# Graph attention layer on sorted edges: four weight and sum buffers, small PSUM operands in one bank, batches of 24 groups

## The chip, the cores and the metric

The kernel runs on one core of one Trainium2 chip. The metric is the device time of one execution in microseconds (us). The kernel before takes 4106.01 us, the median of three runs (4105.14 to 4106.99). A separate execution was taken with the hardware profiler; its times are its own and are given below.

## The reference: what is computed

There are 12,500 nodes with 64 features, and 400,000 edges with 64 features each. The edges are sorted by destination. For every edge an attention score is taken from source, destination and edge features; the scores are normalized by a softmax over all edges that arrive at the same node; the messages are summed with these weights; and each node is updated:

```python
z_att = concat([x[src], x[dst], efeats])
e     = leaky_relu(z_att @ W_attn + b_attn, 0.01)
m     = concat([x[src], efeats]) @ W_ne
alpha = softmax of e over the edges of each dst      # segment max, exp, segment sum
z     = segment_sum(alpha * m, dst)
out   = layernorm(x + relu(concat([x, z]) @ W_out))
```

Because the message is linear, the kernel sums the weighted raw features per node and multiplies by W_ne only at the end.

## The kernel before, in words

**Tiling.** 512 edges are a *group* (128 partitions times T = 4 edges); there are 782 groups. SG = 4 groups are a *chunk*, the unit of loads, scores and sums. BG = 32 groups are a *batch*, the unit of the softmax: its rows are laid out as 128 rows of 128 edges, so at most 32 groups fit. The sizes of the batches are a list: 30, then 23 times 32, then 12 and 4. There are 196 chunks.

**A chunk's load** (`gather`, L134). The edge features `ze` come by one DMA on SP's queue (L140). The source rows `zx` come by one indirect DMA for each 128 edges, 16 for a chunk, all issued by GpSimd, which the profile calls POOL (L149). In the first batch they come from x itself, in all later ones from `table`, a copy of x with the source's share of the score as 65th column. A chunk's `ze` and `zx` live in one of ZB = 11 buffers until the chunk is summed.

**A chunk's score** (`scores`, L155). Sorted destinations fall into a window of S = 48 slots. A matmul (L161) spreads the window's destination scores over 128 partitions into the PSUM tile `win`. VectorE multiplies the edge features by `w_edge`, which lies in the PSUM tile `fixed`, and reduces (L165, L167); adds the source's share (L172, the first to need the gathers); builds the one-hot `hot` of the slots (L174), which also lie in `fixed`; picks the destination's share by product and reduction (L179, L182); and writes the scores `y` (L183, L184). In the first batch the source's share is computed on the way (L169, L171). `hot` has HB = 9 buffers.

**A batch's softmax** (`softmax`, L224). The scores are transposed (L252), and a segmented maximum and sum run as scans along rows. Between rows they pass through the tensor engine: a column becomes one row (`to_row`, L190), is scanned, and goes back (`to_col`, L195 to L200). The result is transposed (L307), and ScalarE writes it to the PSUM tile `alpha` (L309), 128 x 4 x 32.

**A chunk's sums** (`aggregate`, L321). VectorE multiplies `hot` by `alpha` into the edge weights `w` (L324, two buffers); the tensor engine multiplies features by weights, 64 matmuls of 128x64 by 128x48 a chunk, into `pg` (L332, two PSUM banks); VectorE adds each group's 48 columns into the accumulator `acc` at the group's first destination (L342). From the third batch on, `own_part` runs after a chunk until 25 pieces are done: it computes x times W_out for four blocks of 128 nodes, through `pg` as well.

**Start and end.** Before the loop VectorE and ScalarE prepare `table`; the windows' scores are written to `wins` by seven indirect DMAs on POOL (`wk`, L422), which stand among the gathers of the first chunks in POOL's queue. The score of the first chunk waits for the last of them, since its buffers take over their memory. After the last batch, `finish_sorted` (L491) applies the weights, relu and layernorm.

**Order.** The program is written batch by batch: score all chunks, softmax, sum all chunks. A scheduler then orders the instructions on each engine by its own estimates and inserts the semaphores; each engine runs its list strictly in order. Two accesses of different engines to one PSUM tile that lies in one bank are ordered against each other, except where both only read, whatever their columns. [...]before, `fixed`, `pp` (index transposes), `win` and `alpha` hold one each, `sm` (softmax rows) two and `pg` two.

Of the kernel before, what the change touches and what calls it, by code (L numbers as in the profile page):

```python
# [9 lines left out]
F32 = mybir.dt.float32  # L10
# [5 lines left out]
P = 128  # L16
T = 4
# [8 lines left out]
S = 48  # L26
BG = 32
SG = 4
HQ = 4
EW = 65  # L30
ZB = 11
HB = 9
NBC = 4

BF16 = mybir.dt.bfloat16
# [3 lines left out]
def sorted_path(ctx, tc, x, dst, idx, edge, w_ne, w_attn, b_attn, w_out, out, flag):  # L39
# [7 lines left out]
    N, D = x.shape  # L47
# [43 lines left out]
    feats = loop.enter_context(tc.tile_pool(name="feats", bufs=ZB))  # L91
    psum = loop.enter_context(tc.tile_pool(name="psum", bufs=2, space=bass.MemoryType.PSUM))

    fixed = psum.tile([P, S + 2 * D], F32, name="fixed", bufs=1)
    slots = fixed[:, 0:S]
    w_edge = fixed[:, S:S + D].unsqueeze(1)
    w_src = fixed[:, S + D:S + 2 * D].unsqueeze(1)

    def indices(g0, G):

# [33 lines left out]
    def gather(g0, n, srcs, b0, plain):  # L134

        ze = feats.tile([P, SG, T, D], F32, name="ze")
        zx = feats.tile([P, SG, T, EW], F32, name="zx")
        whole = min(n, NG - 1 - g0)
# [16 lines left out]
    def scores(g0, n, ze, zx, drel, b0, y, plain):  # L155

        b = g0 - b0
        wrow = tiny.tile([1, SG, S], F32, name="wrow")
        nc.sync.dma_start(out=wrow[:, 0:n, :], in_=wins[g0:g0 + n, :].unsqueeze(0))
        win = psum.tile([P, SG, S], F32, name="win", bufs=1)  # L160
        nc.tensor.matmul(win[:, 0:n, :], ones_row, wrow[:, 0:n, :], start=True, stop=True)  # L161

        yb = y[:, :, b:b + n].rearrange("p t g -> p g t")
        prod = work.tile([P, SG, T, D], F32, name="prod", bufs=1)
        nc.vector.tensor_tensor(prod[:, 0:n], ze[:, 0:n],  # L165
                                w_edge.unsqueeze(1).to_broadcast([P, n, T, D]), op=OP.mult)
        nc.vector.tensor_reduce(yb, prod[:, 0:n], axis=AX.X, op=OP.add)  # L167
        if plain:
            nc.vector.tensor_tensor(prod[:, 0:n], zx[:, 0:n, :, 0:D],  # L169
                                    w_src.unsqueeze(1).to_broadcast([P, n, T, D]), op=OP.mult)  # L170
            nc.vector.tensor_reduce(zx[:, 0:n, :, D], prod[:, 0:n], axis=AX.X, op=OP.add)  # L171
        nc.vector.tensor_tensor(yb, yb, zx[:, 0:n, :, D], op=OP.add)  # L172
        hot = work.tile([P, SG, T, S], BF16, name="hot", bufs=HB)
        nc.vector.tensor_tensor(  # L174
            hot[:, 0:n], slots.unsqueeze(1).unsqueeze(1).to_broadcast([P, n, T, S]),
            drel[:, :, b:b + n].rearrange("p t g -> p g t").unsqueeze(3).to_broadcast([P, n, T, S]),
            op=OP.is_equal)
        at = work.tile([P, SG, T, D], F32, name="prod", bufs=1)[:, :, :, 0:S]
        nc.vector.tensor_tensor(at[:, 0:n], hot[:, 0:n],  # L179
                                win[:, 0:n].unsqueeze(2).to_broadcast([P, n, T, S]), op=OP.mult)  # L180
        sdst = tiny.tile([P, SG, T], F32, name="sdst")
        nc.vector.tensor_reduce(sdst[:, 0:n], at[:, 0:n], axis=AX.X, op=OP.add)  # L182
        nc.vector.tensor_tensor(sdst[:, 0:n], sdst[:, 0:n], yb, op=OP.add)  # L183
        nc.vector.scalar_tensor_tensor(yb, sdst[:, 0:n], SLOPE, sdst[:, 0:n], op0=OP.mult, op1=OP.max)  # L184
        return hot
# [17 lines left out]
    def neighbours(g0, G):  # L203
# [5 lines left out]
        n = G - 1 if last else G  # L209
        for h in range(HQ):  # L210
            r0 = 0
# [12 lines left out]
    def softmax(G, y, d3, carry, first):  # L224


        R = HQ * G
        far = rows.tile([P, P + 2], F32, name="far3")
# [29 lines left out]
        top = tiny.tile([1, P + 1], F32, name="top")  # L258
# [30 lines left out]
        den = tiny.tile([1, P + 1], F32, name="den")  # L289
# [15 lines left out]
                                sm.rearrange("r (q t) -> r q t", t=T), op=OP.mult)  # L305
        alpha0 = rows.tile([P, T, BG], F32, name="alpha0")
        nc.vector.transpose(alpha0.rearrange("p t g -> p (t g)"), al.rearrange("r t q -> r (t q)"))  # L307
        alpha = psum.tile([P, T, BG], F32, name="alpha", bufs=1)
        nc.scalar.activation(alpha, alpha0, AF.Copy)  # L309
        fac = None  # L310
        if not first:
# [4 lines left out]
            nc.tensor.matmul(pfac[:, 0:1], ones_row, fac1, start=True, stop=True)  # L316
            fac = tiny.tile([P, 1], F32, name="fac")
            nc.vector.tensor_copy(fac, pfac[:, 0:1])
        return alpha, fac, (top[:, R:R + 1], den[:, R:R + 1])

    def aggregate(g0, n, ze, zx, hot, alpha, b0, fac):  # L321
        b = g0 - b0
        w = work.tile([P, SG, T, S], F32, name="w")
        nc.vector.tensor_tensor(  # L324
            w[:, 0:n], hot[:, 0:n],
            alpha[:, :, b:b + n].rearrange("p t g -> p g t").unsqueeze(3).to_broadcast([P, n, T, S]),
            op=OP.mult)
        pg = psum.tile([P, SG, P], F32, name="pg")[:, :, 0:S]
        for g in range(n):
            for t in range(T):  # L330
                for at, z in ((0, ze), (D, zx)):
                    nc.tensor.matmul(pg[at:at + D, g, :], z[:, g, t, 0:D], w[:, g, t, :],  # L332
                                     start=(t == 0), stop=(t == T - 1))
        _, vs = nc.values_load_multi_w_load_instructions(
            d0i[0:1, g0:g0 + n], engines=(EngineType.DVE,), min_val=0, max_val=N - 1,
            skip_runtime_bounds_check_because=within)
        for g in range(n):
            if g == 0 and fac is not None:
                a1 = acc[:, ds(vs[0], 1)]
                nc.vector.tensor_scalar(a1, a1, fac, None, op0=OP.mult)  # L340
            ag = acc[:, ds(vs[g], S)]
            nc.vector.tensor_tensor(ag, ag, pg[:, g, :], op=OP.add)  # L342


    sizes = []
    left = NG
    for short in (SG, 3 * SG):
        sizes.insert(0, short)
        left -= short
    while left > 0:  # L350
        sizes.insert(0, min(left, BG))
        left -= sizes[0]
    starts = [sum(sizes[:k]) for k in range(len(sizes))]

# [22 lines left out]
    with tc.tile_pool(name="pre", bufs=2) as pre:  # L377
        d0f = pre.tile([1, NG], F32, name="d0f", bufs=1)
        nc.vector.tensor_copy(d0f, d0i)
        for g0 in range(0, NG, 3 * P):  # L380
            n = min(3 * P, NG - g0)
# [3 lines left out]
        for c0 in range(0, NB, CB):  # L385
            c1 = min(c0 + CB, NB)
            f1 = min(c1, NFULL)
            n = c1 - c0
# [37 lines left out]
    work = loop.enter_context(tc.tile_pool(name="work", bufs=2))  # L426
# [5 lines left out]
    def own_part(c0):  # L432

        n = min(NBC, NB - c0)
        xb = work.tile([P, NBC, D], F32, name="xb", bufs=1)
        if c0 + n > NFULL:
            nc.vector.memset(xb[:, n - 1, :], 0.0)
            nc.scalar.dma_start(out=xb[0:TAIL, n - 1, :], in_=x[NFULL * P:N, :])
        nf = min(n, NFULL - c0)
        if nf:  # L440
            nc.scalar.dma_start(out=xb[:, 0:nf, :],
                                in_=x[c0 * P:(c0 + nf) * P, :].rearrange("(b p) f -> p b f", p=P))
        xtt = work.tile([D, NBC, P], F32, name="xtt", bufs=1)
        pxt = psum.tile([P, NBC, P], F32, name="pg")
        for j in range(n):
            nc.tensor.transpose(pxt[0:D, j, :], xb[:, j, :], ident)
        nc.scalar.activation(xtt[:, 0:n, :], pxt[0:D, 0:n, :], AF.Copy)  # L447
        po = psum.tile([P, NBC, P], F32, name="pg")[:, :, 0:D]
        for j in range(n):
            nc.tensor.matmul(po[:, j, :], xtt[:, j, :], wout[:, 0, :], start=True, stop=True)  # L450
        xo = work.tile([P, NBC, D], F32, name="xo", bufs=1)
        nc.scalar.activation(xo[:, 0:n, :], po[:, 0:n, :], AF.Copy)
        nc.scalar.dma_start(out=early[c0 * P:(c0 + n) * P, :].rearrange("(b p) f -> p b f", p=P),
                            in_=xo[:, 0:n, :])
# [5 lines left out]
    with loop:  # L460
        carry = None
        own = 0
        ready = {k: prepare(k) for k in range(2)}
        for k, G in enumerate(sizes):
            b0 = starts[k]
            srcs, drel = ready.pop(k)
            d3 = neighbours(b0, G)
            y = rows.tile([P, T, BG], F32, name="y", bufs=2)
            if G < BG:
                nc.vector.memset(y[:, :, G:BG], 0.0)  # L470
            parts = []
            for g0 in range(b0, b0 + G, SG):
                n = min(SG, b0 + G - g0)
                ze, zx = ahead.pop(0) if ahead else gather(g0, n, srcs, b0, k == 0)
                hot = scores(g0, n, ze, zx, drel, b0, y, k == 0)
                parts.append((g0, n, ze, zx, hot))
            if k + 2 < len(sizes):
                ready[k + 2] = prepare(k + 2)
            alpha, fac, carry = softmax(G, y, d3, carry, k == 0)
            for g0, n, ze, zx, hot in parts:  # L480
                aggregate(g0, n, ze, zx, hot, alpha, b0, fac if g0 == b0 else None)
                if own < NB and k > 1:
                    own_part(own)
                    own += NBC
        while own < NB:
            own_part(own)
            own += NBC
# [518 lines left out]
```

## Time and profile before

| | |
|---|---|
| median of three runs | 4106.01 us |
| the profiled execution's own time | 5109.14 us |
| its span, first to last instruction | 5107.4 us |
| tensor engine (PE), matmuls | 1410.6 us busy, 28% |
| VectorE (DVE) | 1708.1 us busy, 33% |
| ScalarE (ACT) | 109.6 us busy, 2% |
| GpSimd (POOL) | 2964.9 us busy, 58% |
| mean granted TensorE clock | 0.547 |
| chain that ended last, by engine | issue 28%, POOL 26%, unknown 19%, DVE 14%, PE 10% |

A line of the timeline gives start, duration, engine, line, operation, output and inputs, and in brackets the idle time of the engine before it with what ended that. A line of the waits gives who waited for whom: total, times and longest, in us. "issue" means that the engine waited for nothing that the profile shows; "remote" means that the releaser is not known. The profiled execution is 1003 us longer than the plain runs.

### The profile page before, as it was taken

What the parts mean: (1) busy time and instruction counts of PE and PEld (TensorE: products, weight loads), DVE (VectorE), ACT (ScalarE), POOL (GpSimd) and SP (SyncE); (2) the same over time, 40 slices, a digit from 0 to 9 for tenths busy, and PEclk for the clock granted to TensorE, in tenths of its full rate; (3) what the DMA queues carried; (4) which work ended last, traced back from release to release, by engine and by line L of the source; (5) the groups of instructions that cost most, each with busy time, mean ns of one, the idle gap of its engine ahead of it and who ended that gap; (6) DMA issues with size and microseconds to landing.
All of it is one profiled execution on the core that took longest, in us unless ns stands there. A gap on an engine that the chain in (4) does not pass through costs nothing.

```text
span 5107.4 us, 39846 instructions
## 1 busy us (share of the span) xinstructions
PE 1410.6 (28%) x14238; PEld 1105.0 (22%) x14238; DVE 1708.1 (33%) x4006; ACT 109.6 (2%) x239; POOL 2964.9 (58%) x3142
## 2 busy tenths in 40 slices
PE   0022233443222222222222222222222222222226
PEld 0012122332222122212121212122222211221225
DVE  3333233232342332332323323323233233233346
ACT  0000000000000000000000000000000000000001
POOL 6645656556556556565565565655655655656550
PEclk9975555555555555555555555555555555555555
DMA  6111122222111112111111111111111211212113
GB/s 145 25 34 42 44 48 54 53 53 60 41 45 44 43 38 48 42 46 41 43 44 43 42 44 43 43 42 44 47 41 40 47 42 38 47 37 48 41 36 77
DMA packets 315273, 239.73 MB, mean 47 GB/s; under 512 B 160576, under 2 KB 264235, under 8 KB 315064
## 3 DMA queue, kind: packets, MB, share of 16 engines
q0 software_dynamic: 100320, 104.41, 10.6%
q1 hardware_dynamic: 147464, 116.22, 8.0%
q10 hardware_dynamic: 67280, 16.45, 1.6%
q8 instruction: 115, 1.88, 0.2%
q14 instruction: 94, 0.77, 0.1%
HBM read 226.98 MB, written 12.28 MB: 47 GB/s over the span
## 4 chain that ended last, share of the span: by engine, by line
issue 28%; POOL 26%; another core or an unknown queue 19%; DVE 14%; PE 10%; DMA 3%; DVEq 1%; ACT 0%; POOLq 0%; ACTq 0%
POOL zx L149 26%; PE pg L332 7%; DMA zx<-table,srcs 2%; DVE y L167 2%; DVE prod L165 2%; DVE sdst L182 1%; DVE prod L179 1%; PE sm L198 1%; PE sm L190 1%; DVE hot L174 1%; DVE w L324 1%; DVE by_row L195 0%; DVE b L271 0%; DVE acc L342 0%
## 5 line engine op out<-in xcount | busy, mean ns | idle before, releaser
L149 POOL DMA_INDIRECT zx<-table,srcs x3008 | 2840.6, 944 | 1951.4 <-issue 841.3
L332 PE MATMUL pg<-w,ze 128*64 128x48 f32 x6256 | 792.3, 297 | 1640.2 <-issue 985.1
L332 PEld LDWEIGHTS pg<-w,ze 128*64 128x64 f32 x6256 | 703.6, 213 | 1729.3 <-issue 1581.7
L332 PE MATMUL pg<-w,zx 128*64 128x48 f32 x6256 | 803.4, 297 | 613.2 <-issue 582.1
L324 DVE TENSOR_TENSOR w<-hot,alpha 128x768 f32<-128x768 bf16 x196 | 184.0, 949 | 2208.2 <-remote 1135.9
L332 PEld LDWEIGHTS pg<-w,zx 128*64 128x64 f32 x6256 | 706.7, 213 | 656.3 <-issue 621.7
L342 DVE TENSOR_TENSOR acc<-acc,pg 128x48 f32 x782 | 153.9, 197 | 812.7 <-remote 742.1
L161 PE MATMUL win<-wrow,ones_row 1*128 1x192 f32 (+1 forms) x392 | 182.0, 552 | 746.8 <-DVE prod L179 433.1
L161 PEld LDWEIGHTS win<-wrow,ones_row 1*128 1x128 f32 x392 | 92.9, 284 | 810.4 <-DVE prod L179 448.3
L165 DVE TENSOR_TENSOR prod<-ze,fixed 128x1024 f32<-128x1024 f32 x196 | 236.9, 1209 | 19.9 <-issue 19.9
L167 DVE TENSOR_REDUCE y<-prod 128x16 f32<-128x1024 f32 x196 | 236.1, 1205 | 2.4 <-DVE y L184 2.3
L182 DVE TENSOR_REDUCE sdst<-prod 128x16 f32<-128x768 f32 x196 | 185.1, 944 | 4.3 <-DVE prod L179 2.4
L179 DVE TENSOR_TENSOR prod<-hot,win 128x768 f32<-128x768 bf16 x196 | 185.4, 946 | 0.9 <-issue 0.2
L174 DVE TENSOR_TENSOR hot<-fixed,drel 128x768 bf16<-128x768 f32 x196 | 185.6, 947 | 0.0
L149 POOL DMA_INDIRECT zx<-in_x_dram,srcs x120 | 116.9, 974 | 51.5 <-issue 36.3
L112 ACT ACTIVATE nat<-raw 32x1024 f32<-32x1024 int32 (+3 forms) x26 | 27.5, 1056 | 3242.2 <-PE pp L115 1762.9
L450 PE MATMUL pg<-wout,xtt 64*128 64x64 f32 x196 | 47.4, 418 | 132.0 <-ACT xtt L447 132.0
L198 PE MATMUL sm<-ones_row,by_row 1*128 1x1 f32 x208 | 59.2, 351 | 81.2 <-DVE by_row L195 66.2
L198 PEld LDWEIGHTS sm<-ones_row,by_row 1*128 1x128 f32 x208 | 50.9, 302 | 131.5 <-DVE by_row L195 104.2
L190 PE MATMUL sm<-order,b 128*1 128x128 f32 x104 | 30.1, 391 | 163.8 <-DVE b L271 158.4
L450 PEld LDWEIGHTS pg<-wout,xtt 64*128 64x128 f32 x196 | 42.8, 319 | 148.3 <-ACT xtt L447 148.3
L190 PE MATMUL sm<-order,s 128*1 128x128 f32 x104 | 30.3, 393 | 147.7 <-issue 57.1
(133 smaller groups left out, 949.1 us busy)
## 6 DMA issues: line engine op xcount, KB each, us to landing
ze<-in_edge_dram SPq DMA_DIRECT2D x194, 512.0 KB
zx<-table,srcs POOLq DMA_INDIRECT x3008
table<-xt ACTq DMA_DIRECT2D x14, 227.5 KB
wrow<-wins SPq DMA_DIRECT2D x195, 0.8 KB
xb<-in_x_dram ACTq DMA_DIRECT2D x24, 128.0 KB
early<-xo ACTq DMA_DIRECT2D x24, 128.0 KB
xb<-in_x_dram ACTq DMA_DIRECT2D x12, 256.0 KB
xo<-early SPq DMA_DIRECT2D x12, 256.0 KB
```

The lines of the kernel that those rows point to most:

```text
L149: nc.gpsimd.indirect_dma_start(out=zx[:, g, t, 0:D] if plain else zx[:, g, t, :], out_offset=None, in_=x[:, :] if plain else table[:, :], ...
L161: nc.tensor.matmul(win[:, 0:n, :], ones_row, wrow[:, 0:n, :], start=True, stop=True)
L165: nc.vector.tensor_tensor(prod[:, 0:n], ze[:, 0:n], w_edge.unsqueeze(1).to_broadcast([P, n, T, D]), op=OP.mult)
L167: nc.vector.tensor_reduce(yb, prod[:, 0:n], axis=AX.X, op=OP.add)
L174: nc.vector.tensor_tensor(hot[:, 0:n], slots.unsqueeze(1).unsqueeze(1).to_broadcast([P, n, T, S]), drel[:, :, b:b + n].rearrange("p t g -> ...
L179: nc.vector.tensor_tensor(at[:, 0:n], hot[:, 0:n], win[:, 0:n].unsqueeze(2).to_broadcast([P, n, T, S]), op=OP.mult)
L182: nc.vector.tensor_reduce(sdst[:, 0:n], at[:, 0:n], axis=AX.X, op=OP.add)
L190: nc.tensor.matmul(p[0:1, :], col, order, start=True, stop=True)
L198: nc.tensor.matmul(p[:, 0:1], by_row, ones_row[:, 0:1], start=True, stop=True)
L324: nc.vector.tensor_tensor(w[:, 0:n], hot[:, 0:n], alpha[:, :, b:b + n].rearrange("p t g -> p g t").unsqueeze(3).to_broadcast([P, n, T, S]) ...
L332: nc.tensor.matmul(pg[at:at + D, g, :], z[:, g, t, 0:D], w[:, g, t, :], start=(t == 0), stop=(t == T - 1))
L342: nc.vector.tensor_tensor(ag, ag, pg[:, g, :], op=OP.add)
```

## The change

- The tiles `win` and `alpha` are no longer PSUM tiles of their own. `fixed` is widened to a whole bank (512 columns) and holds slots, `w_edge`, `w_src`, `alpha` and `win` side by side.
- The two banks that this frees go to `pg`, which has four buffers; `w` has four as well.
- A batch has BS = 24 groups (six chunks). The layout of the softmax keeps its 32 places; the last 8 hold zeros. The sizes are 32 times 24, then 10 and 4. There are still 196 chunks, and 34 batches instead of 26.
- ZB goes from 11 to 10 and HB from 9 to 8.

```diff
+BS = 24
-ZB = 11
-HB = 9
+ZB = 10
+HB = 8
...
-    fixed = psum.tile([P, S + 2 * D], F32, name="fixed", bufs=1)
+    fixed = psum.tile([P, 512], F32, name="fixed", bufs=1)
...
+    alpha = fixed[:, S + 2 * D:S + 2 * D + T * BG].rearrange("p (t g) -> p t g", t=T)
+    win = fixed[:, S + 2 * D + T * BG:S + 2 * D + T * BG + SG * S].rearrange("p (g s) -> p g s", g=SG)
...
-        win = psum.tile([P, SG, S], F32, name="win", bufs=1)
...
-        alpha = psum.tile([P, T, BG], F32, name="alpha", bufs=1)
         nc.scalar.activation(alpha, alpha0, AF.Copy)
...
-        w = work.tile([P, SG, T, S], F32, name="w")
+        w = work.tile([P, SG, T, S], F32, name="w", bufs=4)
...
-        pg = psum.tile([P, SG, P], F32, name="pg")[:, :, 0:S]
+        pg = psum.tile([P, SG, P], F32, name="pg", bufs=4)[:, :, 0:S]
...
-    for short in (SG, 3 * SG):
+    for short in (SG, 10):
         sizes.insert(0, short)
         left -= short
     while left > 0:
-        sizes.insert(0, min(left, BG))
+        sizes.insert(0, min(left, BS))
         left -= sizes[0]
```

The two tiles of `own_part` that share the name `pg` get the same `bufs=4`, and `alpha` is no longer passed from `softmax` to `aggregate`.

More of the change, by code (lines that the diff above doesn't have):

```diff
@@ L318, in softmax, with aggregate @@
             nc.vector.tensor_copy(fac, pfac[:, 0:1])
-        return alpha, fac, (top[:, R:R + 1], den[:, R:R + 1])
-    def aggregate(g0, n, ze, zx, hot, alpha, b0, fac):
+        return fac, (top[:, R:R + 1], den[:, R:R + 1])
+    def aggregate(g0, n, ze, zx, hot, b0, fac):
         b = g0 - b0
-        w = work.tile([P, SG, T, S], F32, name="w")
+        w = work.tile([P, SG, T, S], F32, name="w", bufs=4)
         nc.vector.tensor_tensor(
@@ L443, in own_part @@
         xtt = work.tile([D, NBC, P], F32, name="xtt", bufs=1)
-        pxt = psum.tile([P, NBC, P], F32, name="pg")
+        pxt = psum.tile([P, NBC, P], F32, name="pg", bufs=4)
         for j in range(n):
@@ L447, in own_part @@
         nc.scalar.activation(xtt[:, 0:n, :], pxt[0:D, 0:n, :], AF.Copy)
-        po = psum.tile([P, NBC, P], F32, name="pg")[:, :, 0:D]
+        po = psum.tile([P, NBC, P], F32, name="pg", bufs=4)[:, :, 0:D]
         for j in range(n):
@@ L478, in sorted_path @@
                 ready[k + 2] = prepare(k + 2)
-            alpha, fac, carry = softmax(G, y, d3, carry, k == 0)
+            fac, carry = softmax(G, y, d3, carry, k == 0)
             for g0, n, ze, zx, hot in parts:
-                aggregate(g0, n, ze, zx, hot, alpha, b0, fac if g0 == b0 else None)
+                aggregate(g0, n, ze, zx, hot, b0, fac if g0 == b0 else None)
                 if own < NB and k > 1:
```

## The prediction

> **What bounds the kernel now.** I read the page's busy shares first, then the waits of POOL, then the timeline at the start, in a middle batch and at the end. The profiled execution took 5109.1 us (span 5107.4), the plain runs 4106.0, so the first question is what the profile adds.
>
> ```profile
> PE 1410.6 (28%) x14238; PEld 1105.0 (22%) x14238; DVE 1708.1 (33%) x4006; ACT 109.6 (2%) x239; POOL 2964.9 (58%) x3142
> ...
> L149 POOL DMA_INDIRECT zx<-table,srcs x3008 | 2840.6, 944 | 1951.4 <-issue 841.3
> ```
>
> No engine is near full; POOL, which issues one indirect gather for each 128 edges, comes closest. Its waits:
>
> ```profile
> POOL zx L149 <- issue: 877.5, 2825, 8.4
> POOL zx L149 <- PE pg L332: 786.6, 62, 61.1
> POOL zx L149 <- remote: 252.8, 80, 3.8
> ```
>
> The 877.5 us over 2825 gathers is 0.3 us each: the fixed gap between two gathers. The other two, 1039 us, wait for a buffer that the tensor engine (L332) has to free. They resemble the 1003 us by which the profiled run is too long. Why is PE late? The timeline:
>
> ```profile
> 2410.62 0.24 PE L332 MATMUL pg<-w,ze 128*64 128x48 f32 x1 [1.16 <-issue]
> 2411.32 0.24 PE L332 MATMUL pg<-w,zx 128*64 128x48 f32 x1 [0.46 <-issue]
> 2412.02 0.24 PE L332 MATMUL pg<-w,zx 128*64 128x48 f32 x1 [0.46 <-issue]
> ...
> 2412.17 0.31 PE L332 MATMUL pg<-w,ze 128*64 128x48 f32 x1
> 2412.18 0.31 PE L332 MATMUL pg<-w,zx 128*64 128x48 f32 x1
> 2412.27 0.31 PE L332 MATMUL pg<-w,ze 128*64 128x48 f32 x1
> ```
>
> Sometimes the matmuls come 0.70 us apart and wait for nothing, then a pair takes 0.11 us; a chunk of 64 lasts 3.7 us in one place and 17 in another. VectorE shows the same 0.7 us grid at 223 to 262 us. I take this for the cost of being recorded. Without it a chunk (4 groups, 16 gathers) costs POOL 16 x 1.2485 = 20.0 us (31 gathers from 2522.80 to 2561.51), PE 3.7 and VectorE about 7: **POOL's gathers set the time**, if nothing stops them.
>
> The sum for the plain run. Start:
>
> ```profile
> 196.79 1.22 DVE L165 TENSOR_TENSOR prod<-ze,fixed 128x1024 f32<-128x1024 f32 x1 [19.88 <-issue]
> ...
> 204.73 1.21 DVE L165 TENSOR_TENSOR prod<-ze,fixed 128x1024 f32<-128x1024 f32 x1
> ```
>
> ```profile
> 237.59 0.95 POOL L149 DMA_INDIRECT zx<-table,srcs  x1 [0.30 <-issue]
> 299.67 0.94 POOL L149 DMA_INDIRECT zx<-table,srcs  x1 [61.13 <-PE pg L332]
> ```
>
> POOL fills all 11 buffers (168 gathers) by 238.5 and stands until the first softmax has let PE free one. Scoring advances 7.93 us a chunk, but the starts from 220.59 to 268.40 are 16.1 us later than that pace: recording. So the true restart is 299.7 - 16.1 = 283.6. The other 2960 gathers: 2960 x 1.2485 = 3695.6, to 3979.2. Tail: 2.3 us for the last rows to land, then from L172 at 4993.11 to the last addition at 5036.5, 43.4, then 70.9 to 5107.4: 116.6. Total 4095.8, and 1.7 outside the span: 4097.5 against 4106.0. The sum misses 8.5 us, which I carry along.
>
> **The change, part by part.**
>
> *Number of gathers:* 3128 before and after (96 rather than 120 from x): zero.
>
> *Batches of 24: steady state.* Before, the built order puts the score of the next batch's second chunk (L172) inside the softmax, ahead of the first weights:
>
> ```profile
> 2510.93 0.19 DVE L172 TENSOR_TENSOR y<-y,zx 128x16 f32<-128x16 f32 x1
> ```
>
> Counting from T, the end of a batch's last gather, that instruction can run at T + 40 + 2.3; 11.7 us later (2510.93 to 2522.6) PE frees the first buffer, at T + 54, and POOL needs it at T + 60 (3 buffers ahead): 6 us to spare, no stall. Afterwards nothing of the next batch stands in the softmax; the row at T + 4.5 is transposed, softmax takes 16.7 (from the timeline: transpose to the first column copy 3.7; from the scan at 2504.43 to the weights at 2517.83 13.4, of which 0.4 is that L172), weights and matmuls 4.7, so a buffer is free at T + 26, and with 10 buffers and 6 chunks POOL needs it at T + 80. No stall either. Worth 0; if the 8.5 us are small stalls of the old order in its 24 batches, they go: 0 to -8.5. I take 0, since the rows show slack.
>
> *Eight more softmaxes (34 for 26):* 8 x 16.7 = 134 us of VectorE, also 8 x 8 transposes at L115 (0.29), and on SP's queue 8 more index loads and 32 more of dst; hidden under 119.9 us of gathers a batch. Uncovered, they would add the whole 134.
>
> The Trainium skill (SBUF — State Buffer, "Who interferes with whom") speaks against them: copies and tensor_scalar in VectorE's two-port modes take the port on which GpSimd builds descriptors, and block it. By the rule, 0.20 (L236) and four 0.26 copies (L195) a softmax, 8 x 1.24 = 10 us. The row: 3008 gathers total 2840.6 at a median of 0.944, thus 1 us above the median in all; 8/26 of it is 0.3. I take 0.3, keeping 10 as the end.
>
> *One bank for the small operands.* In the new order each L165 waits for PE's window product, and that product waits for VectorE's last read of the bank, the previous batch's weights among them. So scoring of a batch now begins only after the batch before is weighted, and on PE after its matmuls (outside the batches that also carry x times W_out, where it slips in after the third chunk). The Trainium skill (PSUM — Partial Sum Buffer, "PSUM bank collisions raise a hardware error") demands just this: two engines on one bank and quadrant are to be kept apart by semaphores whatever their addresses. Within a batch it costs nothing visible:
>
> ```profile
> 203.66 1.00 PE L161 MATMUL win<-wrow,ones_row 1*128 1x192 f32 x2 [43.60 <-issue]
> ```
>
> It ends at 204.66, and L165 follows at 204.73 anyhow. By address alone scoring could overlap the matmuls as before; by the rule a batch becomes a serial chain: softmax 16.7, first weights 0.95, six chunks of matmuls 22.1, window 1.0, six scores at 5.3 = 31.8 (L165 and L167 at 1.13, L174, L179 and L182 at 0.87 from start to start, small ones 0.4), end 2.1: 74.7 us against 119.9 of gathers. Both give the same time; the cover is 45 us a batch.
>
> *Four buffers of w and pg:* VectorE's 1136 + 1033 us of waiting at L324 shrink; it was not on POOL's path in the plain run: 0. The 25 x W_out pieces between chunks (four transposes, 0.59 on ScalarE, four matmuls: about 3.1 us) make such a batch's matmuls 41 us, still inside.
>
> *Start.* The last window gather, whose landing starts scoring, is POOL's 134th instead of 138th: 5.0 earlier, 191.8. Six chunks to the transpose: 6 x 7.93 + 1.3 = 48.9, to 240.7; softmax 16.7 + 0.3 = 17.0, to 257.7; weights and matmuls 5.0 (294.7 to 299.67): restart at 262.7, 20.9 earlier. But 160, not 168, gathers are done: + 8 x 1.2485 = 10.0. Net **-10.9**. Were the stretch real, it would be 16.1 before and some 8.5 after: -18.5. So -11 to -18; I take -10.9.
>
> *Tail.* Batches 24, 10, 4; the 10 and the 4 take 69.9 us of gathers after T. Serial: transpose T + 4.5, weights T + 21.5, matmuls to T + 44.5, window T + 45.6, scores 5.3 + 5.3 + 3.1 to T + 59.4, softmax 17 to T + 76.4, 2.5 chunks 10.2 to T + 86.6, window and score 6.3 to T + 92.9, softmax 17, last sums 5.4, to T + 115.3, finish 70.9: T + 186.2, so 116.3 after the last gather. Against 116.6: -0.3. With 2 us of error a batch: -3 to +6.
>
> Sum: 262.7 + 2968 x 1.2485 = 3968.2; + 116.3 + 1.7 = 4086.2; + the unexplained 8.5 + 0.3 = **4095.0**, -0.27%.
>
> **The rivals.**
> *A, more is gained:* the 8.5 us are stalls of the old order with only 6 us of slack, and the stretch is real. For it: the thin slack. Against: every row says slack. 4095 - 8.5 - 7.5 = 4079.
> *B, no change:* the start gain is lost in a tail that is serial now (+6) and in the port (+5 to +10). For it: three softmaxes follow each other there. 4095 + 11 = 4106.
> *C, slower:* the serial chain overtakes the gathers. Place: the six chunks of L332 between softmax and window. It decides at 3.7 + 45 / 6 = 11.2 us a chunk. For it: the profile itself has chunks of 14 to 18 us, and before, eight such chunks (20 us each) stayed hidden, so the old plain time can't exclude 12. Against: 0.11 us a pair wherever the stream is not on the 0.7 us grid. At 12.5 us: 6 x 1.3 = 7.8 a batch, 32 batches: +250, 4345.
>
> **How the numbers follow.** Main case 0.46 (4087 to 4104, of which 0.41 under the bound), A 0.15, B 0.22, C and smaller slowdowns (a stall of a few us a batch somewhere) 0.17. This kernel's runs lie within 0.05%; 0.2% (8.2 us) is about what can be told from no change. Faster (below 4097.8): 0.41 + 0.15 = 0.56. Slower: 0.17 + 0.02 of B's upper end = 0.19. Same: 0.25. Predicted 4095; range 4077 to 4118, which takes in A and B and leaves most of C out.
>
> **What would show it.** Right: POOL's pace again 0.94 + 0.30; its first long wait 10 to 25 us shorter than 61; 34 softmaxes; the first product of a score (L165 here, L167 in the new file) late by under 0.2 us within a batch; the last gather to the end near 137 in the profile. The profiled run should stay near 5100 to 5300, since PE's records (now 1% more) fill it; that says nothing of the time. Wrong: a POOL gap at each batch in a part where matmuls run at 0.11 a pair, or a pace other than 1.2485.

## The result, and the profile after

The changed kernel takes **4081.11 us** (median of four runs, 4080.19 to 4082.37), the kernel before beside it 4106.20 (4105.14 to 4106.99). The ratio is 0.9939, with a 95% interval of 0.9922 to 0.9957: 25.1 us, or 0.61%, are gained. The profiled execution took 4080.57 us, its span is 4078.8. So the 1003 us of the first profile of before are no toll that every recorded execution pays.

The page of the changed kernel, the busy times and the gathers:

```profile
PE 985.2 (24%) x14494; PEld 766.8 (19%) x14494; DVE 1875.2 (46%) x4448; ACT 131.6 (3%) x287; POOL 2967.8 (73%) x3142
...
L152 POOL DMA_INDIRECT zx<-table,srcs x3032 | 2866.8, 946 | 956.7 <-issue 869.6
```

POOL is busy 73% of the span, and the fixed gap between two gathers fills most of the rest. The waits of the changed kernel (who waited for whom: total, times, longest) say the same:

```profile
POOL zx L152 <- issue: 898.3, 2947, 0.3
POOL zx L152 <- DMA zx<-table,srcs: 33.2, 109, 0.3
POOL zx L152 <- PE pg L333: 33.2, 2, 32.9
POOL zx L152 <- DVE srcs L121: 15.2, 1, 15.2
```

Only two waits of a gather are longer than 0.3 us. The one of 15.2 stands before the very first gather, in every trace of the record (15.0 to 15.7). After that POOL stops once, 32.9 us for the first free buffer, and never again. The timeline of the changed kernel shows the places that the prediction's sum goes through: start of scoring, transpose of the first softmax, POOL's restart, last gather.

```profile
191.19 1.22 DVE L167 TENSOR_TENSOR prod<-ze,fixed 128x1024 f32<-128x1024 f32 x1 [49.94 <-DMA wins<-wk]
...
239.18 0.31 DVE L254 STREAM_TRANSPOSE er<-y 128x128 f32<-128x128 f32 x1
```

```profile
260.67 0.94 POOL L152 DMA_INDIRECT zx<-table,srcs  x1 [32.86 <-PE pg L333]
...
3970.51 0.94 POOL L152 DMA_INDIRECT zx<-table,srcs  x1 [0.30 <-issue]
```

They were predicted at 191.8, 240.7 and 262.7; the last gather was to end at 3968.2 and ends at 3971.46. From there to the end it is 107.3 us, where 116.3 were forecast. This stretch is called the tail below. The first profile of before is 1003 us longer than the plain runs, so it can't show what the change moved, and the kernel before was profiled once more.

### The profile page after: what moved, and what is told of

Read it like the earlier page. It is cut to its first block, busy times and chain, and to the rows that moved or that the text cites. A ratio compares the mean times of both kernels' runs of the same rounds, so it can differ in the third digit from the quotient of the medians.

```text
span 4078.8 us, 40728 instructions
## 1 busy us (share of the span) xinstructions
PE 985.2 (24%) x14494; PEld 766.8 (19%) x14494; DVE 1875.2 (46%) x4448; ACT 131.6 (3%) x287; POOL 2967.8 (73%) x3142
## 4 chain that ended last, share of the span: by engine, by line
POOL 41%; DVE 22%; issue 17%; PE 11%; DMA 7%; ACT 1%; DVEq 0%; POOLq 0%; ACTq 0%
POOL zx L152 41%; DMA zx<-table,srcs 7%; PE pg L333 5%; DVE prod L167 3%; DVE y L169 3%; DVE prod L181 3%; PE fixed L163 2%; DVE hot L176 2%; PE sm L200 2%; PE sm L192 2%; DVE acc L343 1%; DVE sdst L184 1%; DVE by_row L197 1%; DVE b L273 1%; DVE w L325 1%
## 5 line engine op out<-in xcount | busy, mean ns | idle before, releaser
L152 POOL DMA_INDIRECT zx<-table,srcs x3032 | 2866.8, 946 | 956.7 <-issue 869.6
L163 PE MATMUL fixed<-wrow,ones_row 1*128 1x192 f32 x392 | 179.0, 553 | 2391.3 <-DVE prod L181 2314.5
L163 PEld LDWEIGHTS fixed<-wrow,ones_row 1*128 1x128 f32 x392 | 88.8, 280 | 2464.9 <-DVE prod L181 2385.1
L333 PE MATMUL pg<-w,ze 128*64 128x48 f32 x6256 | 459.3, 244 | 84.3 <-DVE w L325 73.4
L333 PEld LDWEIGHTS pg<-w,ze 128*64 128x64 f32 x6256 | 449.7, 161 | 104.5 <-DVE w L325 90.1
L333 PE MATMUL pg<-w,zx 128*64 128x48 f32 x6256 | 459.5, 244 | 5.3 <-issue 5.0
L333 PEld LDWEIGHTS pg<-w,zx 128*64 128x64 f32 x6256 | 449.7, 161 | 6.0 <-issue 6.0
L325 DVE TENSOR_TENSOR w<-hot,fixed 128x768 f32<-128x768 bf16 x196 | 176.8, 944 | 42.9 <-PE pg L333 37.7
L181 DVE TENSOR_TENSOR prod<-hot,fixed 128x768 f32<-128x768 bf16 x196 | 185.5, 947 | 0.9
L118 PE MATMUL pp<-ident,nat 24*128 24x24 f32 (+2 forms) x272 | 36.3, 279 | 144.2 <-DVE drel L127 111.4
L174 DVE TENSOR_TENSOR y<-y,zx 128x16 f32<-128x16 f32 x196 | 37.0, 189 | 67.5 <-DMA zx<-table,srcs 64.4
```

What stands on the lines that cost most here:

```text
L152: nc.gpsimd.indirect_dma_start(out=zx[:, g, t, 0:D] if plain else zx[:, g, t, :], out_offset=None, in_=x[:, :] if plain else table[:, :], ...
L181: nc.vector.tensor_tensor(at[:, 0:n], hot[:, 0:n], win[:, 0:n].unsqueeze(2).to_broadcast([P, n, T, S]), op=OP.mult)
L325: nc.vector.tensor_tensor(w[:, 0:n], hot[:, 0:n], alpha[:, :, b:b + n].rearrange("p t g -> p g t").unsqueeze(3).to_broadcast([P, n, T, S]) ...
```

## The experiments

### The kernel before once more

> The kernel before, unchanged, profiled once more. Question: do the 0.70 us grid of its matmuls and the 5109 us belong to that one execution, or to this order of the instructions? If to the execution: about 4106 us in the profile, POOL's gathers 1.25 us apart. Theory S (the gain of the change lies at the start and in the tail alone): POOL has one long wait, of about 45 us after the first softmax, and none later. Theory R (the old order stops the gathers a little in most batches, the serial order does not): besides that one, waits for PE's L332 at 10 or more later batches, 8 to 10 us in sum. If to the order: again near 5100 us.

Measured: 4104.84 us with the profile, span 4103.1. The waits of this second profile of the kernel before, and the place of its one long stop:

```profile
POOL zx L149 <- issue: 912.5, 2994, 0.3
POOL zx L149 <- PE pg L332: 45.1, 1, 45.1
POOL zx L149 <- DMA zx<-table,srcs: 36.9, 121, 0.3
```

```profile
284.29 0.94 POOL L149 DMA_INDIRECT zx<-table,srcs  x1 [45.08 <-PE pg L332]
...
3983.38 0.94 POOL L149 DMA_INDIRECT zx<-table,srcs  x1 [0.30 <-issue]
```

One stop of 45 us after the first gather and no other. The old order with its 6 us of slack stalls nowhere, so theory R has fallen and S stands. The restart at 284.29 is close to the 283.6 that the prediction had worked out of the stretched profile.

Now the 24.3 us between the two spans can be laid out. The restart is 23.6 us earlier; eight gathers fewer are done by then, which takes 10.0 back (8 x 1.25); the other gathers take 0.8 more in all; and the tail, from the end of the last gather (3984.32 before, 3971.46 after), is 107.3 instead of 118.8, 11.5 less.

### The parts of the change, one at a time

Batches of 24 alone:

```diff
+BS = 24
...
-    for short in (SG, 3 * SG):
+    for short in (SG, 10):
...
-        sizes.insert(0, min(left, BG))
+        sizes.insert(0, min(left, BS))
```

> Batches of 24 (32 times 24, then 10 and 4) in the kernel before; banks, two buffers of w and pg, ZB 11 and HB 9 stay. Theory S: six chunks are scored before the first softmax instead of eight, so the restart comes about 21 us earlier, and with 11 buffers 176 gathers are done by then instead of 168, 10 us more: 4106 - 31 = 4075 us, and less by whatever the tail gives (up to 9): 4066 to 4075. That would be below the changed kernel (4081), which lost two chunks of buffers to make room. Theory R: the small stalls stay as the order is not serial: 4075 or above, with waits of POOL at many batches.

Measured: 4084.69 us, ratio 0.9945 (0.9931 to 0.9958), no other stop of POOL than the one for the first free buffer. That agrees with S, but the time is 10 us above its sum. In this kernel, the old order puts the next batch's scores into the first softmax: the timeline of VectorE shows three of them between the transpose and the first weights.

```profile
242.04 0.30 DVE L253 STREAM_TRANSPOSE er<-y 128x128 f32<-128x128 f32 x1
242.26 1.18 DVE L168 TENSOR_REDUCE y<-prod 128x16 f32<-128x1024 f32 x1
247.42 1.20 DVE L168 TENSOR_REDUCE y<-prod 128x16 f32<-128x1024 f32 x1
253.72 1.20 DVE L168 TENSOR_REDUCE y<-prod 128x16 f32<-128x1024 f32 x1
260.31 1.20 DVE L168 TENSOR_REDUCE y<-prod 128x16 f32<-128x1024 f32 x1
268.28 1.82 DVE L325 TENSOR_TENSOR w<-hot,alpha 128x768 f32<-128x768 bf16 x2
```

(The L168 at 242.26 ends a score begun before, so four L168 stand there.) The transpose-to-weights stretch is 26.2 us here, 19.5 in the kernel before and 16.5 in the changed one, where the one bank keeps scores out. So the restart is at 273.25 and not at 262. The tail is 113.2 us: the new batch sizes alone take 5.6 from the 118.8 of before.

The first batch alone at 24, all else as before:

```diff
+    sizes.insert(0, 6)
+    left -= 6 + 24
     while left > 0:
         sizes.insert(0, min(left, BG))
         left -= sizes[0]
+    sizes.insert(0, 24)
```

> The kernel before with its first batch at 24 groups instead of 30 (24, 23 times 32, 6, 12, 4), all else unchanged. Theory S: the whole gain of the start, -21 for six chunks instead of eight and -10 for 176 gathers instead of 168: 4075 us, plus or minus 5 for one more batch in the tail. Theory R: the same start, as R speaks of the middle only, and the small waits of POOL at its batches of 32 remain to be seen in the profile. If neither: the start isn't on the path that sets the end, 4106.

Measured: 4083.03 us, ratio 0.9939 (0.9926 to 0.9953). One shorter batch at the start gives what 32 of them give. Of the smaller batches, only the first earns anything, and the eight more softmaxes cost nothing that is seen.

One bank and four buffers, with ZB 10 and HB 8, but the old batches:

```diff
-BS = 24
+BS = 32
...
-    for short in (SG, 10):
+    for short in (SG, 3 * SG):
```

> The changed kernel with the old batches (30, 23 times 32, 12 and 4): one bank, four buffers of w and pg, ZB 10 and HB 8. Theory S: eight chunks before the first softmax as before, 152 gathers done at the stop instead of 168: 16 x 1.25 = 20 us later, less 5 for the earlier last window gather: about 4121 us, 4112 if the shorter tail comes from the order. Theory R: the serial order takes away 8 to 10 us of stalls in the middle: 4103 to 4112, and no wait of POOL after the first softmax.

Measured: 4109.67 us, ratio 1.0006 (0.9997 to 1.0014): no gain by itself. The time lies in R's window and 2 us below S's, so it doesn't choose between them; the waits do, and they speak for S. The trace holds effects of opposite sign. POOL has only 152 gathers to do before it stops, 16 fewer, which costs 20.0 us, but it restarts 5.7 us earlier than before (278.60), since no score stands in the softmax:

```profile
278.60 0.94 POOL L152 DMA_INDIRECT zx<-table,srcs  x1 [60.71 <-PE pg L333]
```

And the tail is 109.3 instead of 118.8 us, with the same last batches, 9.5 less. Together that is 4.8 more, as the spans say (4107.9 and 4103.1). The serial order is the likely reason for the shorter tail; this kernel also has four buffers and fewer `zx` buffers, and only the four buffers can be ruled out (the next kernel has two and a tail of 105.6).

The change with two buffers of w and pg:

```diff
-        w = work.tile([P, SG, T, S], F32, name="w", bufs=4)
+        w = work.tile([P, SG, T, S], F32, name="w", bufs=2)
...
-        pg = psum.tile([P, SG, P], F32, name="pg", bufs=4)[:, :, 0:S]
+        pg = psum.tile([P, SG, P], F32, name="pg", bufs=2)[:, :, 0:S]
```

(the two other tiles named `pg` as well)

> The changed kernel with two buffers of w and pg instead of four; one bank, batches of 24, ZB 10 and HB 8 stay. Theory: the buffers change nothing of POOL's pace and nothing of the first release (the first chunk's matmuls need one buffer); they shorten the sums of a batch from about 19 us to 15.5, which counts in the tail alone, after its last two batches: 4081 + 1 to 5 us = 4082 to 4086. Rival: the four buffers are what makes the stage fast enough to hide; then waits of POOL in the middle and over 4090.

Measured: 4075.64 us, ratio 0.9931 (0.9917 to 0.9944), so rather below the change than above it, and below the forecast of 4082 to 4086: that sums would take longer with two buffers, and lengthen the tail, did not come true. POOL's stop is the same:

```profile
260.68 0.94 POOL L152 DMA_INDIRECT zx<-table,srcs  x1 [32.83 <-PE pg L333]
```

The four buffers bring nothing, and they take room that ZB 11 and HB 9 had. The profiles put the 4.9 us between the spans in two places: the gathers take 3.1 us less in sum (2863.7 against 2866.8), the tail 1.7 less (105.6 for 107.3). For 2.8 of the 3.1 the traces have a reason, shown under "The port" below.

### The stop itself

If the one stop of POOL is where the time lies, then moving the start of scoring must move the time one for one. Scoring starts when the last of the seven `wk` gathers has been written to `wins`. With two buffers of `wk` a third gather can go only after the first has been written, and in POOL's order they stand in pairs, 11 us apart, with eight gathers of `zx` between two pairs. With seven buffers they can go one behind the other.

```diff
-            wk = pre.tile([P, S], F32, name="wk")
+            wk = pre.tile([P, S], F32, name="wk", bufs=NW)
```

In the changed kernel:

> The changed kernel with seven buffers of wk instead of two, so that the seven window gathers need not wait for each other's write to wins and stand in POOL's queue one after the other: the last goes at about 156 us instead of 186. Theory (the only stop of POOL is the one before the first release, and each us of it counts): scoring starts 30 us earlier, at 161, the first release comes at 231 instead of 261, POOL's wait shrinks from 32.9 us to about 3, and the time falls by 30 to 4051. Rival (the gain comes from the middle or the tail): 4076 or more.

Measured: **4052.70 us**, ratio 0.9872 (0.9857 to 0.9887). The forecast was 4051. The restart is 29.8 us earlier, and the time is 28.4 less than that of the change. POOL hardly stops:

```profile
230.92 0.94 POOL L152 DMA_INDIRECT zx<-table,srcs  x1 [2.85 <-PE pg L333]
```

The same edit in the kernel before:

> The kernel before with seven buffers of wk and nothing else changed. Theory: scoring starts 30 us earlier, POOL's one wait of 45 us shrinks to about 15, and the time falls by 30 to 4076: as much as the whole change brought, or more. Rival (the start is not on the path): 4106.

Measured: 4084.61 us, ratio 0.9950 (0.9937 to 0.9964): 20 us less and not 30. Scoring does start 31.0 us earlier (166.51 for 197.47), but VectorE then runs into an index copy that the new order put into the first score, and it waits there for the gathers that read the buffer:

```profile
179.79 0.29 DVE L118 CAST srcs<-pp 128x128 int32<-128x128 f32 x1 [7.55 <-DMA zx<-in_x_dram,srcs]
```

31.0 less 7.6 is 23.4, and the restart is 23.2 earlier (261.08). This one line of diff in the old kernel is worth four fifths of the whole change.

### How much cover the serial chain has

```diff
+        for again in range(4):
+            for g in range(n):
+                for t in range(T):
+                    for at, z in ((0, ze), (D, zx)):
...
```

> The changed kernel with the matmuls of L333 done four times (the last pass, with a new start, gives the sums): a chunk costs the tensor engine 7.4 us at the pace of the middle (1.85), or 14.8 at that of the start (3.7). Theory (a batch's chain has about 50 us of cover under its gathers, so a chunk may last about 11 us): six times 5.6 is hidden in the middle, the first release is 11 us later and the tail some 10 to 25 us longer: 4100 to 4120. Rival (the chain is close to the gathers' pace): 32 batches of 20 us or more each: above 4700.

Measured: 4150.98 us, ratio 1.0114 (1.0098 to 1.0129). The middle hides all of it: besides the one stop, now 38.7 us, POOL never waits more than 0.3 after its first gather, and its last gather ends at 3976.5, 5 us later. The other 65 us are in the tail (172.3 for 107.3). I had sized it at 10 to 25, counting mainly the last two short batches; the last batch of 24 with its six chunks stands there as well. In the middle of this kernel:

```profile
2402.08 3.52 DVE L325 TENSOR_TENSOR w<-hot,fixed 128x768 f32<-128x768 bf16 x4
...
2467.94 0.26 DVE L121 CAST srcs<-pp 128x96 int32<-128x96 f32 x1 [39.23 <-DMA zx<-table,srcs]
...
2521.89 3.52 DVE L325 TENSOR_TENSOR w<-hot,fixed 128x768 f32<-128x768 bf16 x4
```

The weights of two batches are 119.8 us apart, the gathers' pace. Six chunks of 7.47 us after 2402.1 end near 2448, and the next scores begin only when a gather lets the index copy go at 2467.9. So about 20 us are left, and a chunk could last 7.5 + 20 / 6 = 10.8 us; the prediction's figure was 11.2. This is reckoned from the trace, not run.

### Four kernels on a chip that behaves otherwise

The last four kernels ran together, on a chip other than the two of the experiments above. On it **the kernel before takes 5129.37 us** (5125.06 to 5136.70), near the 5109.14 of its first profile. The ratios are to that time. It is called the slow chip here; each chip was used on one occasion only, so whether the chip or the occasion makes the difference is not known.

The change with two buffers, ZB 11 and HB 9:

```diff
-ZB = 10
-HB = 8
+ZB = 11
+HB = 9
...
-        w = work.tile([P, SG, T, S], F32, name="w", bufs=4)
+        w = work.tile([P, SG, T, S], F32, name="w", bufs=2)
...
-        pg = psum.tile([P, SG, P], F32, name="pg", bufs=4)[:, :, 0:S]
+        pg = psum.tile([P, SG, P], F32, name="pg", bufs=2)[:, :, 0:S]
```

(the two other tiles named `pg` as well)

> The changed kernel with two buffers of w and pg, and with the room that this gives used for ZB 11 and HB 9 again; one bank and batches of 24 stay. Theory (each gather done before POOL's stop counts in full): 176 gathers instead of 160 by the stop, the same first release at 261, POOL's wait 12.8 us instead of 32.8: 20 us below the kernel with two buffers (4075.6), 4056. Rival (the first chunks' order changes with the room, or the stop is not what counts): 4070 or more.

Measured: 5611.49 us, ratio 1.0936 (1.0921 to 1.0951).

That kernel with the old batches, so that the one bank is the only difference from the kernel before:

> The one bank for the small PSUM operands alone: batches of 30, 32, ..., 12, 4, two buffers of w and pg, ZB 11 and HB 9 as before. Theory: its order keeps the next batch's scores out of the first softmax (first release at 278.6 instead of 284.3) and out of the tail (109 us instead of 119 after the last gather): 4105 - 15 = 4090 us, 20 below the kernel with the bank, four buffers and ZB 10 (4109.7). Rival (the bank as such costs, by the serial order): 4105 or more.

Measured: 5629.05 us, ratio 1.0971 (1.0956 to 1.0986).

That of ZB 11 with seven `wk` and the last batches 10 and 4 made one of 14:

> All that has helped so far: one bank, batches of 24 (32 of them, and one last of 14 in place of 10 and 4), two buffers of w and pg, ZB 11 and HB 9, seven buffers of wk. Theory: first release at about 231, before POOL has filled the 11 buffers at 248, so no stop at all: 32.8 us off the kernel with two buffers (4075.6), 4043; one batch at the end instead of two saves about 3: 4040, with POOL's gathers without a gap from 17 to 3937. Rival (another wait takes the stop's place): 4050 or more.

Measured: 5578.35 us, ratio 1.0875 (1.0860 to 1.0890).

The matmuls eight times:

> The changed kernel with the matmuls of L333 done eight times (the last pass gives the sums), 14.9 us a chunk at 1.867 a pass. By the prediction a batch's chain overtakes its gathers at 11.2 us a chunk, by the profile of the changed kernel (1.87 + 54 / 6) at about 10.9. Theory: six chunks are 22 to 24 us too long in each of 32 batches, 700 to 780, and start and tail add some 160 more: 4940 to 5030 us, with a wait of POOL at each batch. Rival (the cover is thinner, or the next batch's scores don't overlap at all): over 5100; (thicker): under 4600.

Measured: 8424.73 us, ratio 1.6423 (1.6400 to 1.6445).

None of the four expectations can be judged by these times, as they were worked out for a chip on which the kernel before takes 4105. What the four show is what is slow on this one. In the kernel with eightfold matmuls, the tensor engine has more to do than POOL, so POOL gathers for 20 us a chunk and then stands. Four stretches of it, taken by turns without and with gathers (start and end, length, busy time and instructions of PE, its weight loads, VectorE, ScalarE and POOL, granted clock, DMA share, GB/s):

```profile
4060.00:4072.00 12.00, 12.00 (x410) 12.00 (x408) 0.00 (x0) 0.00 (x0) 0.00 (x0) 0.98 0.02 4
4076.00:4092.00 16.00, 4.61 (x37) 3.41 (x38) 0.00 (x0) 0.00 (x0) 12.04 (x14) 0.55 0.24 49
4098.00:4110.00 12.00, 12.00 (x364) 12.00 (x362) 0.00 (x0) 0.00 (x0) 0.00 (x0) 0.86 0.01 3
4114.00:4130.00 16.00, 4.41 (x34) 3.23 (x34) 0.00 (x0) 0.00 (x0) 12.11 (x13) 0.53 0.22 37
```

Without gathers 410 matmuls in 12 us, with them 37 in 16: less than a tenth of the pace. The timeline gives the moment. The gathers start again at 4073.89; until 4074.9 the matmuls come in pairs 0.058 us apart, and then they thin out:

```profile
4078.20 0.33 PE L334 MATMUL pg<-w,zx 128*64 128x48 f32 x1 [1.08 <-issue]
...
4079.64 0.24 PE L334 MATMUL pg<-w,zx 128*64 128x48 f32 x1 [0.98 <-issue]
...
4094.57 0.24 PE L334 MATMUL pg<-w,ze 128*64 128x48 f32 x1 [1.17 <-issue]
4095.97 0.24 PE L334 MATMUL pg<-w,ze 128*64 128x48 f32 x1 [1.16 <-issue]
```

The last gather of this chunk starts at 4092.61, its last packet lands at 4094.7, and from 4096.7 on the pairs are dense again. The load of the edge features, which starts with the gathers, is not needed for it: its last packet here lands at 4077.1. On another chip, the kernel with fourfold matmuls streams beside gathers that never pause, and keeps 7.47 us for the 256 matmuls of a chunk (the view of L334 alone: PE, its weight loads, clock, DMA share, GB/s):

```profile
2000.00:2400.00 400.00, 143.56 (x4608) 142.62 (x4608) 0.67 0.23 53
```

The program alone does not explain this, since the kernel before, unchanged, takes 4105 us on one chip and 5129 on another.

The first profile of before, which I had in hand, shows the same. There the matmuls crawl from 2388.93 to 2412.02 and are dense from 2412.17; POOL's last gather ahead of that started at 2406.07, its last packet landed at 2408.2, and POOL stood until 2413.64. No edge features were loaded between 2386.4 and 2414.4.

So in both traces a crawl of the matmuls ends soon after the gathers do. That the gathers cause it is not shown, and two things in the first profile of before say that it is not so simple. The burst of matmuls that ends in this crawl began dense, 0.11 us a pair from 2386.52 to 2388.16, although gathers had been running since 2367.37. And VectorE's start was slow too (the grid at 223 to 262 us of the prediction), 22 us of it after the last packet of a gather, at 239.7, with POOL standing until 299.67:

```profile
242.82 0.95 DVE L182 TENSOR_REDUCE sdst<-prod 128x16 f32<-128x768 f32 x1 [1.75 <-remote]
244.92 0.18 DVE L183 TENSOR_TENSOR sdst<-sdst,y 128x16 f32<-128x16 f32 x1 [1.15 <-DVE sdst L182]
...
258.92 0.19 DVE L183 TENSOR_TENSOR sdst<-sdst,y 128x16 f32<-128x16 f32 x1 [1.85 <-remote]
```

The traces of the slow chip have such a stretch too. Before it, and in the second profile of before, L182 and L183 follow each other 0.98 to 0.99 us apart, from start to start. What makes the engines slow, and why on one chip only, is open. A toll of recording that only this chip pays is not excluded either.

What it does to the kernel is plain. With 37 matmuls in 16 us the 64 of a chunk don't keep up with its gathers (20 us). POOL then stands because the tensor engine has not freed a buffer, and while it stands the tensor engine catches up.

And it turns the verdict. There three kernels with one bank lose 9 to 10%, and the one in which the bank is the only difference loses most. In the one with ZB 11 and the old `wk`, the scores and the softmax of a batch come after the matmuls of the batch before, and POOL stops at every batch:

```profile
3127.10 0.94 POOL L152 DMA_INDIRECT zx<-table,srcs  x1 [31.79 <-PE pg L333]
3173.90 0.95 POOL L152 DMA_INDIRECT zx<-table,srcs  x1 [7.08 <-PE pg L333]
...
3295.32 0.95 POOL L152 DMA_INDIRECT zx<-table,srcs  x1 [31.91 <-PE pg L333]
```

From one stop of 32 us to the next it is 168.2 us for six chunks, against 119.9 of gathers alone. Over the whole run, from the restart to the last gather, it is 27.8 us a chunk, and 25.2 in the first profile of before, which stops too. The changed kernel as it stands was not run there, nor was the kernel with seven `wk`. That they lose there too is likely, since they have the same serial order; it is not shown.

## Why the prediction was right or wrong

**The sum: right mechanism, 13.9 us too high.** Predicted were 4095.0, measured 4081.1. The start accounts for 2.7 of it and the tail for 11.2. The measured time lies inside the range, 4 us above its lower end.

**What sets the time: right.** POOL's gathers do, with a single stop. Their pace was 1.2485 us by a short stretch; over the 2960 gathers of the second profile of before it is 1.2501, and they take 4.5 us more than the sum had. This, a tail of 118.8 for 116.6 and a restart 0.7 later make 7.4 of the 8.5 us that the sum missed. They were sizes, not stalls, so it was right to carry them over to the changed kernel.

**Start: right mechanism, a little small.** Forecast -10.9 (restart -20.9, fewer gathers +10.0); measured -23.6 and +10.0, thus -13.6.

**Tail: the term that was mis-sized.** The prediction put it at -0.3, from 116.6 to 116.3. It is -11.5: 2.2 because the tail of before is 118.8, and the rest because that of the changed kernel is 107.3 and not 116.3. I had taken 22.1 us for the matmuls of six chunks at 0.11 us a pair, which is the pace of a burst that has just begun. In the middle of the changed kernel a pair soon takes 0.058, where the granted clock goes from 0.50 to 1.00 (start and end, length, PE, weight loads, VectorE, ScalarE, POOL, clock, DMA share, GB/s):

```profile
2385.50:2389.00 3.50, 3.42 (x64) 3.42 (x66) 2.62 (x4) 0.00 (x0) 2.77 (x3) 0.50 0.20 41
2390.00:2392.00 2.00, 2.00 (x76) 2.00 (x74) 1.16 (x3) 0.00 (x0) 1.39 (x3) 1.00 0.69 184
```

From the first weights to the next batch's scores it is 15.4 us (2504.43 to 2519.82), not 24. So the chain was not late at the end: the batch of 10 waited for its last gather (L174 at 3953.07, after 2.40 us of idle), where my sum had it six us behind. The new order does most of it, as far as the parts tell: 9.5 us in the kernel with the bank and the old batches, 5.6 in the one with the new batches alone, 11.5 with both.

**Steady state and eight more softmaxes: right, 0.** No wait over 0.3 us after the restart; one short first batch does as much as 32.

**Four buffers: right, 0**, if not a small loss.

**The port: small, as forecast, but its size is not measured.** Forecast +0.3. What gathers take over 945 ns each sums to 6.0 us before and 6.7 after, +0.7, but this is no price of eight softmaxes: the same sum is 3.4 in the kernel with two buffers, which has as many of them. The rule of the Trainium skill (SBUF — State Buffer, "Who interferes with whom"), that a copy or a tensor_scalar of VectorE in a two-port mode and GpSimd block each other, does show here, in the changed kernel:

```profile
2619.28 1.12 POOL L152 DMA_INDIRECT zx<-table,srcs  x1 [0.30 <-issue]
```

```profile
2619.56 0.20 DVE L238 TENSOR_SCALAR same<-pf 128x128 f32<-128x128 f32 x1
```

and does not in the kernel with two buffers:

```profile
2616.07 0.95 POOL L152 DMA_INDIRECT zx<-table,srcs  x1 [0.30 <-issue]
```

```profile
2616.57 0.20 DVE L238 TENSOR_SCALAR same<-pf 128x128 f32<-128x128 f32 x1
```

What differs is the moment. In these two traces, where L238 starts 0.21 to 0.29 us after the gather, the gather takes 1.05 to 1.12; where it starts 0.44 us after it or later, the gather takes 0.94 to 0.97. The changed kernel has 20 of the first kind and the one with two buffers 3, and that is 2.8 us of the 3.1 by which their gathers differ. The copies of L197 that lie inside a gather all leave it at 0.94. So the 10 us that I had kept as the rule's end counted copies that cost nothing here, and a full price for every tensor_scalar.

**One bank: the serial chain has its cover**, 10.8 us a chunk by the fourfold matmuls against my 11.2.

**"The cost of being recorded": wrong.** This was the step on which the plain run stood. Recorded executions of the kernel before (4104.84) and of the changed kernel (4080.57) have no such grid, so it is no toll of recording as such; and the kernel before also takes 5129 us on one chip in nine executions. On which chip the first profile was taken is not known. The forecast held all the same, since the plain times that it was made for came from executions without this. Three of the signs named in the prediction were read off the stretched profile and fell with it: 5100 to 5300 us for the profiled run, 137 us for the tail (107.3), and a stop 10 to 25 us shorter than 61 (28.2 shorter than that, 12.2 shorter than the 45.1 of the second profile).

**The rivals.** A was nearer (4079) than the main case, by a wrong cause: there were no stalls of the old order and no real stretch. B's losses did not come. C, the one on the other side, had the right place: on the slow chip a chunk takes some 21.6 us (weights at 3005.63 and 3027.24 in the kernel with ZB 11) and the one-bank kernels are slower. Its price was too high: 6 x (21.6 - 11.2) = 62 us a batch by its formula, 48.3 measured (168.2 less 119.9), and against the kernel before, which stops there too, only the 482 us of the whole run (5611.49 less 5129.37), 15 a batch. I had argued against it with the dense stretches of the profile; the ones that I showed, from 2412.17 on, lay where POOL stood.

## What to carry to other kernels

Where one engine sets the pace and stops only once, look for what ends that stop: here seven small tiles in place of two, one line, gave more (28.4 us on top of the change) than buffers, bank and batch size together (25.1); in the kernel before, where another wait stepped in, it gave 20.3. When a profile is far longer than the plain runs, don't set it aside as recording before the same program has been profiled again elsewhere, and lay the slow stretches of one engine beside the activity of the others: that the matmuls crawl beside gathers could be read from the first trace. An order that lets stages run one after the other may be free on one chip and cost 9 to 10% on another, so its cover is to be known before it is taken.

## What the runs showed of the hardware that was not expected

- On one chip the matmul stream falls to less than a tenth beside indirect gathers (37 in 16 us against 410 in 12), while on another the same kind of stream is not touched (4608 in 400 us). The crawl begins 1 to 2.5 us into the stretch that the two share, and ends 4 us after the last gather has started (6 in the first profile of before), 2 to 4 us after its last packet. VectorE was slow on that first profile too, also without gathers. The cause is open.
- The pace of small fp32 matmuls (128x64 by 128x48) goes with the granted clock: pairs 0.11 us apart at 0.50, 0.058 at 1.00, which comes 3.5 to 4.7 us after a burst or a dense stretch has begun (2505.42 to 2508.9 in the changed kernel, 4096.7 to 4101.4 in the eightfold one). Fourfold matmuls raised the mean granted clock from 0.588 to 0.725.
- A 0.20 us tensor_scalar of VectorE can lengthen an indirect gather (0.944) to 1.05 to 1.12 us, and whether it does goes with the moment at which it starts: 0.21 to 0.29 us after the gather it did, 0.44 us or later it did not, in the changed kernel and in the one with two buffers. The moment is not the whole of it: with batches of 24 alone, two gathers with the operation 0.25 and 0.27 us in took 0.95 and 0.97.
